# A causal convolution with 28 block products a tile in place of 31, and an S4 response whose tables move through the array

## The chip, the cores and the metric

The kernel runs on one core of one Trainium2 chip, as one launch. The time is the device time of one execution in microseconds, lower is better. A profile is one execution recorded by the hardware profiler; times inside it count from its first instruction. TensorE (PE) multiplies, VectorE (DVE) and ScalarE (ACT) work on what it leaves in PSUM, GpSimd (POOL) works on SBUF, and SyncE (SP) issues most DMAs.

## What is computed

One "macaron" layer on 2048 tokens of 1024 channels, all in float32: a feed-forward with 4-bit weights, a long convolution (S4), and the same feed-forward again.

```python
x = x + 0.5 * ffn(layernorm(x))        # ffn: silu(x @ Wg) * (x @ Wu) @ Wd, weights dequantized from 4 bits
x = x + s4(layernorm(x))
x = x + 0.5 * ffn(layernorm(x))

# s4, with L = 1024 and K the S4 response of length L, the same for all rows:
K = ifft(at_roots, L).real
y = irfft(rfft(u, n=2 * L) * rfft(K, n=2 * L), n=2 * L)[..., :L]
return y + D[0] * u
```

The S4 step is a causal convolution of each token's 1024 channels with K. With channels in eight blocks of 128 it is a block Toeplitz product: output block `i` is the sum over `j <= i` of input block `j` times T(i - j), where T(0) to T(7) are 128x128 matrices made from K.

## The kernel before

Tokens are worked in four blocks of 512 (four tiles of 128 each). `JOBS` lists eight feed-forwards, two for each block of tokens; the convolution of a block stands inside the job that follows its first feed-forward.

A job is `gate_up` and then `down`. `gate_up` runs 64 steps: eight waves of up to six PSUM accumulators (`pg`, units of 128 columns), eight groups of 128 input channels a wave. In a step each unit gets two products (L558): one with the float16 rest of the input (`xTl`), one with its high part (`xTh`). After each step but a wave's last, each accumulator is rescaled in place by the ratio of two quantization scales, by ScalarE for even units (L523) and by VectorE for odd ones (L525). After a wave's last step ScalarE makes `g` (L581), VectorE `hf` (L584, two buffers), and GpSimd splits that into `hh` (L586) and `hl` (L588). `down` works likewise with `po`.

Other work hangs on the steps as hooks. For the block of the job before, tile `t` is normalized at step 8 + 4t (L192), transposed in two halves at 10 + 4t (`turn_whole`, giving `st`), and convolved at 12 + 4t (`convolve`); in the first set all of that is 30 steps later, since the S4 tables come first (`s4_tables`, one piece a step of the second job). A scheduler of the language then puts the instructions of each engine in an order of its own, so the products of a convolution can be mixed with those of a step; an engine works through its queue in that order.

PSUM has eight banks: six accumulators and a pool of two (`bank`, tag `ps`), which transposes, convolution and tables share in turn. A bank can be written again when the engine that reads it is done.

`convolve` takes the lower four output blocks straight: four products, each of one input block with a run of `toeplitz`, in one bank (L898), which VectorE adds to `x` (L906). The upper four are done by pairs of blocks: GpSimd adds neighbouring input blocks (`sums`, L910), and three kinds of products (with `toeplitz` itself, and with `after` and `ahead`, differences of neighbouring T) fill a second bank, added at L933; those with `sums` fill a third, added to both blocks of a pair (L936). That is 31 block products in 17 instructions. A float32 product is recorded as two matmuls, each with its own weight load, so a group of 16 products counts x32.

`s4_response` (L829 to L852) makes K: 16 products, each with a 128x128 table (stride of eight columns) as weights and one column as moving operand, give K as 128 rows of eight, which are written to DRAM behind 127 zeros. `s4_toeplitz` reads that back so that row `p` is shifted by `p` (L869), turns the rows round with one product for each half (L872) and makes `toeplitz`, `after` and `ahead`.

Of the kernel before, what the change touches and what calls it, by code (L numbers as in the profile page):

```python
# [9 lines left out]
F32 = mybir.dt.float32  # L10
# [6 lines left out]
ALU = mybir.AluOpType  # L17
# [5 lines left out]
P = 128  # L23
HID = 1024
INTER = 2752
TOK = 2048
TB = 512
NT = TB // P
NC = HID // P
# [23 lines left out]
def macaron_s4_kernel(  # L53
# [31 lines left out]
    nc = tc.nc  # L85
# [4 lines left out]
    const = ctx.enter_context(tc.tile_pool(name="const", bufs=1))  # L90
# [7 lines left out]
    ypool = ctx.enter_context(tc.tile_pool(name="y", bufs=4))  # L98
# [4 lines left out]
    def bank(name):  # L103
        return ppool.tile([P, 512], F32, tag="ps", name=name)
# [4 lines left out]
    def t4(name):  # L109
        return xpool.tile([P, HID], F32, tag="x", name=name)  # L110

    def t2(name, dt=F32):
        return hpool.tile([P, 512], dt, tag="h", name=name)
# [28 lines left out]
    x = {}  # L142
# [376 lines left out]
    h = {}  # L519
# [125 lines left out]

    toeplitz = const.tile([P, HID], F32, tag="toeplitz", name="toeplitz")

    blocks = toeplitz.rearrange("p (d m) -> p d m", d=NC)  # L650
    after = const.tile([P, 3, P], F32, tag="after", name="after")
    ahead = const.tile([P, 3, P], F32, tag="ahead", name="ahead")
    k_dram = dpool.tile([1, P - 1 + HID], F32, tag="k", name="k_dram")
    s4 = {}

# [173 lines left out]
    def s4_response():  # L829

        tables = [t4("s4_tc"), t4("s4_ts")]
        for i in range(2):
            nc.sync.dma_start(tables[i], c_dft[:, i, :])
        ps = bank("s4_k")
        for r in range(8):
            for i in range(2):
                nc.tensor.matmul(
                    ps[:, r : r + 1],
                    tables[i].rearrange("p (a r) -> p r a", r=8)[:, r, :],
                    s4["se"][:, i, r : r + 1],  # L840
                    start=(i == 0),
                    stop=(i == 1),
                )
        k = t4("s4_response")
        d, none = k[:1, 8:9], k[:1, P : 2 * P - 1]
        nc.sync.dma_start(d, dskip.unsqueeze(0))
        nc.gpsimd.memset(none, 0.0)
        nc.vector.tensor_scalar(k[:, :8], ps[:, :8], 1.0 / HID, None, ALU.mult)
        nc.vector.tensor_tensor(k[:1, 0:1], k[:1, 0:1], d, ALU.add)
        nc.sync.dma_start(k_dram[:, : P - 1], none)  # L850
        nc.sync.dma_start(k_dram[0, P - 1 :].rearrange("(a r) -> a r", r=8), k[:, :8])
        s4.clear()  # L852

    def s4_toeplitz():

        both = [t4("s4_rows"), t4("s4_turn")]
        rows, turn = both[0], both[1][:, :P]
        nc.gpsimd.memset(turn, 0.0)
        nc.gpsimd.affine_select(
            out=turn,  # L860
            in_=turn,
            pattern=[[1, P]],
            compare_op=ALU.not_equal,
            fill=1.0,
            base=1 - P,
            channel_multiplier=1,
        )
        first = k_dram[:]
        nc.sync.dma_start(rows, bass.AP(first.tensor, first.offset, [[1, P], [1, HID]]))  # L869
        for i in range(NH):  # L870
            ps = bank(f"s4_t{i}")
            nc.tensor.matmul(ps, turn, rows[:, bass.ts(i, 512)], start=True, stop=True)  # L872
            dst = toeplitz[:, bass.ts(i, 512)]
            if i:
                nc.vector.tensor_copy(dst, ps)
            else:
                nc.scalar.copy(dst, ps)
        for dst, d in ((after, 3), (ahead, 1)):
            nc.vector.tensor_tensor(dst, blocks[:, d : d + 5 : 2], blocks[:, 2:7:2], ALU.subtract)

    def s4_tables():

        yield from s4_poles()
        yield
        yield from s4_roots()
        yield
        s4_response()
        yield
        s4_toeplitz()

    def convolve(b, t, s, name):

        ps = bank(f"pc_{name}_0")
        for c in range(4):
            nc.tensor.matmul(  # L898
                ps[:, P * c :],
                s[:, c, :],  # L900
                toeplitz[:, : 512 - P * c],
                start=(c == 0),
                stop=(c == 3),
            )
        part = x[b][t][:, :512]
        nc.vector.tensor_tensor(part, part, ps, ALU.add)  # L906

        sums = ypool.tile([P, TB], F32, tag="y", name=f"sums_{name}")
        sums = sums[:, : 3 * P].rearrange("p (c t) -> p c t", c=3)
        nc.gpsimd.tensor_tensor(sums, s[:, 0:6:2, :], s[:, 1:6:2, :], ALU.add)  # L910
        own = bank(f"pc_{name}_1")
        both = bank(f"pc_{name}_2")[:, : 2 * P].rearrange("p (y m) -> p y m", y=2)
        flat = own.rearrange("p (y m) -> p y m", y=4)
        upper, lower = flat[:, 0:4:2], flat[:, 1:4:2]

        def product(dst, lhsT, rhs, start=False, stop=False):
            nc.tensor.matmul(dst, lhsT, rhs, start=start, stop=stop, skip_group_check=True)  # L917

        for y in range(2):
            product(flat[:, 2 * y : 2 * y + 2], s[:, 4 + 2 * y, :], blocks[:, 0:2], start=(y == 0))  # L920
        for y in range(2):
            product(flat[:, 2 * y + 1], s[:, 5 + 2 * y, :], blocks[:, 0])
        for i in range(3):
            y = slice(max(0, i - 1), 2)
            d = slice(max(0, 1 - i), 3 - i)
            product(lower[:, y], s[:, 2 * i, :], after[:, d])
            product(upper[:, y], s[:, 2 * i + 1, :], ahead[:, d], stop=(i == 2))
        for i in range(3):
            y = slice(max(0, i - 1), 2)
            d = slice(2 * max(1, 2 - i), 2 * (3 - i) + 1, 2)  # L930
            product(both[:, y], sums[:, i, :], blocks[:, d], start=(i == 0), stop=(i == 2))
        part = x[b][t][:, 512:]
        nc.vector.tensor_tensor(part, part, own, ALU.add)  # L933
        part = part.rearrange("p (y h m) -> p y h m", y=2, h=2)
        twice = both.unsqueeze(2).to_broadcast([P, 2, 2, P])
        nc.vector.tensor_tensor(part, part, twice, ALU.add)  # L936

    def turn_whole(n, name):
        s = t4(name).rearrange("p (c t) -> p c t", c=NC)
# [12 lines left out]
    def general():  # L952
# [193 lines left out]
        for b in range(TOK // TB):  # L1146
            load_x(b, rows_of(u, b))
            feed_forward(b, 1)
            moments(b, 2)
            deviations(b, 2)  # L1150
            for t in range(NT):
                s = turn_whole(normalized(b, t), f"gt_{b}_{t}")
                convolve(b, t, s, f"g{b}_{t}")
            feed_forward(b, 3)
            for t, dst in enumerate(rows_of(out, b)):
                nc.sync.dma_start(dst, x[b][t])
            x.pop(b)
# [6 lines left out]
    def fast():  # L1164
        for j, (b, k) in enumerate(JOBS):
# [7 lines left out]
            if prev:  # L1173
# [3 lines left out]
                if pk == 1:  # L1177
# [11 lines left out]
                    def conv(t):  # L1189
                        convolve(pb, t, s4x.pop(t), f"{pb}_{t}")  # L1190
# [210 lines left out]
```

## Time and profile before

| | us |
|---|---|
| median of 4 runs | 2212.37 |
| lowest, highest | 2209.86, 2213.68 |
| the profiled execution | 2209.96 |
| its span, first to last instruction | 2208.2 |
| TensorE busy in it | 2123.3 |
| VectorE busy in it | 1702.4 |
| the 16 convolved tiles stand at | 465 to 518, 662 to 724, 1437 to 1499, 1713 to 1775 |
| the S4 response on TensorE | 423.8 to 433.5 |

Busy time is the time in which an engine has at least one instruction under way. Lengths of matmuls overlap, so the pace of TensorE is read from the starts. Idle time in brackets is that of the engine just before the instruction, with what ended it.

### The profile page before, as it was taken

To read this page: it belongs to the slowest core of one execution; us is meant where nothing else is said; L and a number is where in the kernel's file an instruction comes from. 1 tells how busy PE (TensorE), PEld (TensorE's weight loads), DVE (VectorE), ACT (ScalarE), POOL (GpSimd) and SP (SyncE) were. 2 spreads that over 40 slices of the span, in tenths; PEclk is the share of its full clock that TensorE was granted. 3 is DMA by queue.
4 is the path that set the end of the run, shared out by engine and by line. 5 is a ranking of instruction groups with operands and counts; after the bars stand their busy time and mean duration, and the time that the engine had idled before them with its cause. 6 is when DMAs were issued, how large, how long until landed. Compare 5 with 4: busy or idle time off the path is not lost.

```text
span 2208.2 us, 27967 instructions
## 1 busy us (share of the span) xinstructions
PE 2123.3 (96%) x9524; PEld 1416.3 (64%) x9524; DVE 1702.4 (77%) x2803; ACT 1425.0 (65%) x2245; POOL 367.5 (17%) x389
## 2 busy tenths in 40 slices
PE   5888899999999999999999999999999999999998
PEld 3454575566867558655785558676586765865576
DVE  7777968777786877778877788867788677777776
ACT  5677776555764577666766667646776467766675
POOL 0222302121011220122102220112201122012210
PEclk9999999999999999999999999999999999999999
DMA  7778774434453545644655455534445354564443
GB/s 246 250 244 283 240 252 150 140 103 154 138 156 115 169 134 157 192 142 123 206 172 163 127 169 138 153 115 157 135 137 153 115 177 136 155 196 142 132 132 121
DMA packets 163669, 359.93 MB, mean 163 GB/s; under 512 B 22395, under 2 KB 27572, under 8 KB 163518
## 3 DMA queue, kind: packets, MB, share of 16 engines
q1 hardware_dynamic: 162670, 356.50, 53.0%
q8 instruction: 78, 1.28, 0.2%
q10 hardware_dynamic: 592, 1.16, 0.1%
q0 software_dynamic: 256, 0.39, 0.1%
q14 instruction: 73, 0.60, 0.1%
HBM read 306.86 MB, written 50.73 MB: 162 GB/s over the span
## 4 chain that ended last, share of the span: by engine, by line
PE 54%; issue 24%; DVE 4%; POOL 4%; ACT 1%; DMA 1%; SPq 0%; POOLq 0%; DVEq 0%; ACTq 0%
PE pg L558 32%; PE po L620 16%; PE pc L917 3%; POOL hl L588 3%; DVE hf L584 2%; PE pc L898 1%; POOL hh L586 1%; DVE pg L525 1%; PE pb L641 1%; PE st L199 1%; PE pt L199 0%; ACT g L581 0%; DVE po L525 0%; DMA wd<-wdq 0%; DVE qd L470 0%
## 5 line engine op out<-in xcount | busy, mean ns | idle before, releaser
L523 ACT ACTIVATE pg<-pg,rat 128x512 f32<-128x512 f32 x1264 | 799.8, 660 | 475.9 <-PE pg L558 469.6
L525 DVE TENSOR_TENSOR pg<-pg,rat 128x512 f32<-128x512 f32 x1144 | 763.9, 694 | 184.1 <-PE pg L558 179.9
L558 PE MATMUL pg<-xTh,w 128*128 128x512 f32 x2752 | 882.0, 445 | 21.6 <-DVE hf L584 11.9
L558 PE MATMUL pg<-xTl,w 128*128 128x512 f16 x2752 | 745.4, 384 | 17.0 <-DMA w<-wq 9.3
L558 PEld LDWEIGHTS pg<-xTh,w 128*128 128x128 f32 x2752 | 521.0, 190 | 208.0 <-DVE hf L584 24.3
L620 PE MATMUL po<-hl,wd 128*128 128x512 f32 x1344 | 539.4, 403 | 13.1 <-DVE po L525 8.4
L523 ACT ACTIVATE po<-po,ratd 128x512 f32<-128x512 f32 x670 | 437.5, 662 | 166.4 <-PE po L620 166.0
L620 PE MATMUL po<-hh,wd 128*128 128x512 f32 x1344 | 524.6, 392 | 0.0
L525 DVE TENSOR_TENSOR po<-po,ratd 128x512 f32<-128x512 f32 x610 | 420.7, 697 | 99.5 <-PE po L620 95.3
L558 PEld LDWEIGHTS <-w 128*128 128x128 bf16 x2752 | 227.7, 99 | 360.2 <-issue 183.9
L586 POOL CAST hh<-hf 128x512 fp32r<-128x512 f32 x168 | 109.5, 652 | 1534.8 <-DVE hf L584 1452.2
L620 PEld LDWEIGHTS po<-hl,wd 128*128 128x128 f32 x1344 | 252.5, 188 | 91.7 <-DVE po L525 22.3
L620 PEld LDWEIGHTS po<-hh,wd 128*128 128x128 f32 x1344 | 253.7, 189 | 45.9
L588 POOL TENSOR_TENSOR hl<-hf,hh 128x512 fp32r<-128x512 f32 x168 | 222.2, 1322 | 13.4
L584 DVE SCALAR_TENSOR_TENSOR hf<-pg,rat,g 128x512 f32<-128x512 f32 x168 | 121.8, 746 | 92.4 <-ACT g L581 56.8
L581 ACT ACTIVATE g<-pg,rat 128x512 f32<-128x512 f32 x168 | 106.9, 686 | 64.2 <-PE pg L558 63.8
L162 DVE BATCH_NORM_STATS2 stats<-x 128x6 f32<-128x512 f32 x96 | 63.6, 677 | 1.1
L199 PE MATMUL pt<-ident,xn 128*128 128x128 f32 x256 | 43.0, 285 | 10.8 <-ACT xn L1269 10.8
L222 DVE TENSOR_TENSOR xTl<-pt,xTh 128x512 f16<-128x512 f32 x56 | 38.3, 688 | 14.2 <-ACT xTh L221 14.0
L643 DVE TENSOR_TENSOR x<-x,pb 128x512 f32<-128x512 f32 x64 | 43.2, 678 | 5.9 <-PE pb L641 5.0
L199 PEld LDWEIGHTS pt<-ident,xn 128*128 128x128 f32 x256 | 33.5, 147 | 21.3 <-ACT xn L1269 12.5
L641 PE MATMUL pb<-ident,y 128*128 128x128 f32 x256 | 42.5, 279 | 3.0 <-DVE x L643 2.9
(151 smaller groups left out, 808.6 us busy)
## 6 DMA issues: line engine op xcount, KB each, us to landing
w<-wq SPq DMA_DIRECT2D x319, 384.0 KB
wd<-wdq SPq DMA_DIRECT2D x336, 256.0 KB
w<-wq SPq DMA_DIRECT2D x128, 256.0 KB
w<-wq SPq DMA_DIRECT2D x64, 320.0 KB
x<-in_L_attn_u_dram SPq DMA_DIRECT2D x30, 512.0 KB
wq<-q SPq DMA_DIRECT2D x40, 384.0 KB
wdq<-qd SPq DMA_DIRECT2D x32, 256.0 KB
xs<-x SPq DMA_DIRECT2D x16, 512.0 KB
```

What stands on the lines that cost most here:

```text
L162: nc.vector.bn_stats(stats[:, t, i, :], x[b][t][:, bass.ts(i, 512)])
L199: nc.tensor.transpose(ps[:, bass.ts(k, P)], n[:, bass.ts(k, P)], ident)
L523: nc.scalar.activation(dst, src, AF.Copy, scale=sc)
L525: nc.vector.tensor_tensor(dst, src, sc.to_broadcast([P, TB]), ALU.mult)
L558: nc.tensor.matmul(p, weights, (lo, hi)[k][:, g, :], start=(g == 0 and not done), stop=(g == GK - 1 and done), skip_group_check=True,)
L581: nc.scalar.activation(g, pg, AF.Silu, scale=rat[:, 2 * f, GK - 1 :])
L584: nc.vector.scalar_tensor_tensor(hf, pu, last, g, ALU.mult, ALU.mult)
L586: nc.gpsimd.tensor_copy(hi, hf)
L588: nc.gpsimd.tensor_tensor(lo, hf, hi.bitcast(F32), ALU.subtract)
L620: nc.tensor.matmul(ps[c], w[:, bass.ts(c, P)], part, start=(f == 0 and k == 0), stop=(f == NF - 1), skip_group_check=True,)
L641: nc.tensor.transpose(ps[:, bass.ts(c, P)], yT[a, c][:, bass.ts(t, P)], ident)
L917: nc.tensor.matmul(dst, lhsT, rhs, start=start, stop=stop, skip_group_check=True)
```

## The change

`toeplitz` goes as a constant; in its place are `near` (T(0), T(1), T(2), T(4)), `after` and `ahead` with four blocks each, and `middle` (T(2) - T(4) and T(6) - T(4)). The lower four output blocks are now done by pairs too, and in the upper four the pairs with a whole distance between them are done by pairs of pairs, with further sums of input blocks. Each half uses a bank `pc` for what belongs to one block and a bank `pb` for what goes to several; VectorE adds five times a tile.

The response is made as one row: the one column is the weight, the table is the moving operand, 128 columns a product, in two banks; K then goes to DRAM as one row of 4 KB.

```diff
-    toeplitz = const.tile([P, HID], F32, tag="toeplitz", name="toeplitz")
-    blocks = toeplitz.rearrange("p (d m) -> p d m", d=NC)
-    after = const.tile([P, 3, P], F32, tag="after", name="after")
-    ahead = const.tile([P, 3, P], F32, tag="ahead", name="ahead")
+    near = const.tile([P, 4, P], F32, tag="near", name="near")
+    after = const.tile([P, 4, P], F32, tag="after", name="after")
+    ahead = const.tile([P, 4, P], F32, tag="ahead", name="ahead")
+    middle = const.tile([P, 2, P], F32, tag="middle", name="middle")
...
-        ps = bank("s4_k")
-        for r in range(8):
-            for i in range(2):
-                nc.tensor.matmul(
-                    ps[:, r : r + 1],
-                    tables[i].rearrange("p (a r) -> p r a", r=8)[:, r, :],
-                    s4["se"][:, i, r : r + 1],
...
+        for half in range(2):
+            ps = bank(f"s4_k{half}")
+            for r in range(4):
+                for i in range(2):
+                    nc.tensor.matmul(
+                        ps[:1, bass.ts(r, P)],
+                        s4["se"][:, i, 4 * half + r : 4 * half + r + 1],
+                        tables[i].rearrange("p (a r) -> p r a", r=8)[:, 4 * half + r, :],
...
-        nc.sync.dma_start(k_dram[0, P - 1 :].rearrange("(a r) -> a r", r=8), k[:, :8])
+        nc.sync.dma_start(k_dram[:, P - 1 :], k[:1])
...
+        nc.vector.tensor_copy(near[:, 0:3], blocks[:, 0:3])
+        nc.vector.tensor_copy(near[:, 3], blocks[:, 4])
         for dst, d in ((after, 3), (ahead, 1)):
-            nc.vector.tensor_tensor(dst, blocks[:, d : d + 5 : 2], blocks[:, 2:7:2], ALU.subtract)
+            own = dst[:, 0:3]
+            nc.vector.tensor_tensor(own, blocks[:, d : d + 5 : 2], blocks[:, 2:7:2], ALU.subtract)
+            nc.vector.tensor_tensor(dst[:, 3], dst[:, 2], dst[:, 1], ALU.subtract)
+            nc.vector.tensor_tensor(dst[:, 2], dst[:, 0], dst[:, 1], ALU.subtract)
+        for i in range(2):
+            src = blocks[:, 2 + 4 * i]
+            nc.vector.tensor_tensor(middle[:, i], src, blocks[:, 4], ALU.subtract)
...
+        nc.gpsimd.tensor_tensor(sums[:, 0:3], s[:, 0:6:2, :], s[:, 1:6:2, :], ALU.add)
+        nc.gpsimd.tensor_tensor(quad, s[:, 0:2, :], s[:, 2:4, :], ALU.add)
+        nc.gpsimd.tensor_tensor(sums[:, 3], sums[:, 0], sums[:, 1], ALU.add)
...
+        for o in range(2):
+            own = bank(f"pc_{name}_{o}")
+            flat = own.rearrange("p (d m) -> p d m", d=4)
+            mine = s[:, 4 * o : 4 * o + 4]
+            product(flat[:, 0:2], mine[:, 0], near[:, 0:2], start=True)
+            product(flat[:, 1], mine[:, 1], near[:, 0])
+            product(flat[:, 2:4], mine[:, 2], near[:, 0:2])
+            product(flat[:, 3], mine[:, 3], near[:, 0])
+            product(flat[:, 3], mine[:, 0], after[:, 0])
+            product(flat[:, 2], mine[:, 1], ahead[:, 0], stop=(o == 0))
+            both = bank(f"pb_{name}_{o}")
+            if o == 0:
+                product(both[:, :P], sums[:, 0], near[:, 2], start=True, stop=True)
+            else:
+                for y in range(2):
+                    product(flat[:, 2 * y + 1], s[:, 2 - 2 * y], after[:, 2 + y])
+                    product(flat[:, 2 * y], s[:, 3 - 2 * y], ahead[:, 2 + y], stop=(y == 1))
+                twice = both.rearrange("p (y m) -> p y m", y=4)
+                product(twice[:, 0], sums[:, 1], middle[:, 0], start=True)
+                product(twice[:, 1], sums[:, 0], middle[:, 1])
+                product(twice[:, 1], sums[:, 2], near[:, 2])
+                for y in range(2):
+                    product(twice[:, y], sums[:, 3], near[:, 3])
+                product(twice[:, 3], quad[:, 0], after[:, 1])
+                product(twice[:, 2], quad[:, 1], ahead[:, 1], stop=True)
+            part = x[b][t][:, bass.ts(o, 512)]
+            nc.vector.tensor_tensor(part, part, own, ALU.add)
+            part = part.rearrange("p (y h m) -> p y h m", y=2, h=2)
+            if o == 0:
+                part = part[:, 1]
+                add = both[:, :P].unsqueeze(1).to_broadcast([P, 2, P])
+                nc.vector.tensor_tensor(part, part, add, ALU.add)
+            else:
+                add = twice[:, 0:2].unsqueeze(2).to_broadcast([P, 2, 2, P])
+                nc.vector.tensor_tensor(part, part, add, ALU.add)
+                add = twice[:, 2:4].unsqueeze(1).to_broadcast([P, 2, 2, P])
+                nc.vector.tensor_tensor(part, part, add, ALU.add)
```

In the changed kernel the add of `pc` is L949, that of the first `pb` L954, those of the second L957 and L959.

More of the change, by code (lines that the diff above doesn't have):

```diff
@@ L833, in s4_response @@
             nc.sync.dma_start(tables[i], c_dft[:, i, :])
-        ps = bank("s4_k")
-        for r in range(8):
-            for i in range(2):
-                nc.tensor.matmul(
-                    ps[:, r : r + 1],
-                    tables[i].rearrange("p (a r) -> p r a", r=8)[:, r, :],
-                    s4["se"][:, i, r : r + 1],
[L841 to L845, printed above, removed]
+        k, rest = t4("s4_response"), t2("s4_rest")
+        d, none = rest[:1, :1], rest[:1, 1:P]
         nc.sync.dma_start(d, dskip.unsqueeze(0))
         nc.gpsimd.memset(none, 0.0)
-        nc.vector.tensor_scalar(k[:, :8], ps[:, :8], 1.0 / HID, None, ALU.mult)
+        for half in range(2):
[6 more added lines that the diff above has]
+                        tables[i].rearrange("p (a r) -> p r a", r=8)[:, 4 * half + r, :],
+                        start=(i == 0),
+                        stop=(i == 1),
+                    )
+            nc.vector.tensor_scalar(
+                k[:1].rearrange("p (a r) -> p r a", r=8)[:, 4 * half : 4 * half + 4],
+                ps[:1].rearrange("p (r a) -> p r a", r=4),
+                1.0 / HID,
+                None,
+                ALU.mult,
+            )
         nc.vector.tensor_tensor(k[:1, 0:1], k[:1, 0:1], d, ALU.add)
         nc.sync.dma_start(k_dram[:, : P - 1], none)
-        nc.sync.dma_start(k_dram[0, P - 1 :].rearrange("(a r) -> a r", r=8), k[:, :8])
+        nc.sync.dma_start(k_dram[:, P - 1 :], k[:1])
         s4.clear()
     def s4_toeplitz():
-        both = [t4("s4_rows"), t4("s4_turn")]
-        rows, turn = both[0], both[1][:, :P]
+        rows, turn, whole = t4("s4_rows"), t4("s4_turn")[:, :P], t4("s4_whole")
         nc.gpsimd.memset(turn, 0.0)
@@ L872, in s4_toeplitz @@
             nc.tensor.matmul(ps, turn, rows[:, bass.ts(i, 512)], start=True, stop=True)
-            dst = toeplitz[:, bass.ts(i, 512)]
+            dst = whole[:, bass.ts(i, 512)]
             if i:
@@ L877, in s4_toeplitz @@
                 nc.scalar.copy(dst, ps)
+        blocks = whole.rearrange("p (d m) -> p d m", d=NC)
+        nc.vector.tensor_copy(near[:, 0:3], blocks[:, 0:3])
+        nc.vector.tensor_copy(near[:, 3], blocks[:, 4])
         for dst, d in ((after, 3), (ahead, 1)):
-            nc.vector.tensor_tensor(dst, blocks[:, d : d + 5 : 2], blocks[:, 2:7:2], ALU.subtract)
+            own = dst[:, 0:3]
[5 more added lines that the diff above has]
+            nc.vector.tensor_tensor(middle[:, i], src, blocks[:, 4], ALU.subtract)
     def s4_tables():
@@ L891, in convolve @@
     def convolve(b, t, s, name):
[L896 to L906, printed above, removed]
-        sums = ypool.tile([P, TB], F32, tag="y", name=f"sums_{name}")
-        sums = sums[:, : 3 * P].rearrange("p (c t) -> p c t", c=3)
@@ L910, in convolve @@
[L910 to L914, printed above, removed]
+        sums = ypool.tile([P, TB], F32, tag="y", name=f"sums_{name}")
+        sums = sums.rearrange("p (c t) -> p c t", c=4)
+        quad = ypool.tile([P, TB], F32, tag="y", name=f"quad_{name}")
@@ L916, in product @@
+        quad = quad[:, : 2 * P].rearrange("p (c t) -> p c t", c=2)
+        nc.gpsimd.tensor_tensor(sums[:, 0:3], s[:, 0:6:2, :], s[:, 1:6:2, :], ALU.add)
+        nc.gpsimd.tensor_tensor(quad, s[:, 0:2, :], s[:, 2:4, :], ALU.add)
+        nc.gpsimd.tensor_tensor(sums[:, 3], sums[:, 0], sums[:, 1], ALU.add)
         def product(dst, lhsT, rhs, start=False, stop=False):
             nc.tensor.matmul(dst, lhsT, rhs, start=start, stop=stop, skip_group_check=True)
-        for y in range(2):
-            product(flat[:, 2 * y : 2 * y + 2], s[:, 4 + 2 * y, :], blocks[:, 0:2], start=(y == 0))
@@ L921, in convolve @@
[L921 to L936, printed above, removed]
+        for o in range(2):
[35 more added lines that the diff above has]
+                nc.vector.tensor_tensor(part, part, add, ALU.add)
```

## The prediction

> **What bounds the kernel now.** I read the page first: TensorE is busy for 96% of the span, VectorE for 77%.
>
> ```profile
> PE 2123.3 (96%) x9524; PEld 1416.3 (64%) x9524; DVE 1702.4 (77%) x2803; ACT 1425.0 (65%) x2245; POOL 367.5 (17%) x389
> ```
>
> So a change pays if it shortens TensorE's own queue and adds no wait to it. Next the timeline around one of the 16 convolved tiles (TensorE, then VectorE). Columns: start, length, engine, line, what, count.
>
> ```profile
> 662.37 2.32 PE L898 MATMUL pc<-toeplitz,st 128*128 128x512 f32 x8
> 664.53 1.47 PE L917 MATMUL pc<-toeplitz,st 128*128 128x256 f32 x8
> 665.84 0.60 PE L917 MATMUL pc<-after,st 128*128 128x256 f32 x2
> 666.27 0.60 PE L917 MATMUL pc<-ahead,st 128*128 128x256 f32 x2
> ...
> 667.57 0.39 PE L917 MATMUL pc<-after,st 128*128 128x128 f32 x2
> 667.79 0.39 PE L917 MATMUL pc<-ahead,st 128*128 128x128 f32 x2
> 668.01 1.25 PE L917 MATMUL pc<-toeplitz,sums 128*128 128x256 f32 x6
> 669.10 0.81 PE L558 MATMUL pg<-xTl,w 128*128 128x512 f16 x3
> ```
>
> ```profile
> 664.73 0.69 DVE L906 TENSOR_TENSOR x<-x,pc 128x512 f32<-128x512 f32 x1 [1.29 <-PE pc L898]
> 665.45 0.69 DVE L162 BATCH_NORM_STATS2 stats<-x 128x6 f32<-128x512 f32 x1
> 668.21 0.69 DVE L933 TENSOR_TENSOR x<-x,pc 128x512 f32<-128x512 f32 x1 [2.07 <-PE pc L917]
> ```
>
> Starts, not lengths, give the pace: a product of 256 columns takes 0.433 us (665.84 to 666.27), one of 128 takes 0.22 (667.57, 667.79, 668.01). The tile occupies TensorE from 662.37 to 669.10, 6.73 us for 31 blocks, without a gap: the bank of L898 is added by VectorE while L917 runs in the other bank. VectorE begins that add 0.42 us after the start of the last L898 product (664.31) and ends at 665.42.
>
> Half of the later tiles look different: the step ahead of them ends a wave, and VectorE first owes three `hf` products, the third of which waits for GpSimd.
>
> ```profile
> 680.60 1.41 DVE L584 SCALAR_TENSOR_TENSOR hf<-pg,rat,g 128x512 f32<-128x512 f32 x2 [1.47 <-ACT g L581]
> 683.40 0.75 DVE L584 SCALAR_TENSOR_TENSOR hf<-pg,rat,g 128x512 f32<-128x512 f32 x1 [1.40 <-POOL hl L588]
> 684.07 0.68 DVE L906 TENSOR_TENSOR x<-x,pc 128x512 f32<-128x512 f32 x1
> ```
>
> That convolution starts at 680.77, so its first bank is free only 3.98 us later. Before, nothing needs the bank until the last group of products at 686.41.
>
> **The change part by part: products of a tile.** 17 products become 24: four of 256 columns, 20 of 128. 4 x 0.433 + 20 x 0.22 = 6.13 us against 6.73: 0.6 us less a tile, 16 tiles, 9.6 us if nothing waits.
>
> Narrow products in long runs are new: before, at most two follow each other. The nearest row is L764: 16 weight loads of 128 columns, each with a product of 8 columns, start 0.111 us apart, and a 128-column f32 product is two such loads, so 0.22 holds. I take it. The Trainium skill (TensorE: Matmul & The Clock Gate, Back-to-back issue gap) says the spacing of load and product pairs is set by both, and gives 81 ns a pair at 128 columns where the product alone would take about 56. By that ratio 20 products would take 6.4 us instead of 4.4 and the tile would lose; this trace's 0.22 beside 0.433 does not agree.
>
> **The two banks.** A tile now uses four banks out of a pool of two: `pc_0`, `pb_0`, `pc_1`, `pb_1`. `pc_1` can't start until VectorE has added `pc_0` (L949). The built program's order of instructions shows what stands between: the one product of `pb_0` and three gate/up products (five or six in the tiles behind a wave's end). On TensorE the weight stream queues behind that wait. Per tile, from the tile's first product:
>
> Ten tiles (four in the first set, six later): `pc_0` takes 2 x 0.433 + 4 x 0.22 = 1.75; its last product starts at 1.53, the add runs 0.42 later, 1.95 to 2.64; releases by VectorE reach TensorE 0.06 later (hf L584 ends at 441.44, the product starts at 441.49), so 2.70. TensorE has work until 1.75 + 0.22 + 3 x 0.2155 = 2.62. Wait 0.08. Then `pc_1` 2 x 0.433 + 8 x 0.22 = 2.63 and `pb_1` 7 x 0.22 = 1.54: done at 6.87. Before, the same work (tile and three products) took 6.73 + 0.65 = 7.38. Gain 0.5.
>
> Six tiles behind a wave's end: VectorE's queue puts the add behind the three `hf`, as before, so it ends at 3.98, and `pc_1` starts at 4.04. TensorE has work until 1.75 + 0.22 + 5 x 0.2155 = 3.05. Wait 1.0. Done at 4.04 + 2.63 + 1.54 = 8.21, against 6.73 + 5 x 0.2155 = 7.81. Loss 0.4.
>
> Sum: -10 x 0.5 + 6 x 0.4 = -2.6 us. Most of the gain goes into the wait.
>
> `pb_1` needs the add of `pb_0` (256 columns, under 0.69 us, behind L949): ready by 3.4, needed at 5.3. No wait.
>
> **VectorE and GpSimd.** Adds go from three to five a tile (four of 0.69, one of 256 columns), up to 1.1 us more of VectorE. Between two tiles TensorE runs some 48 products and transposes, about 11 us; VectorE has 12 rescales, a copy, a normalization, statistics and two adds there, 0.6 to 0.7 us each when back to back (the statistics at 665.45 follow the add at 664.73), some 10.5 us. It fits, with under 1 us to spare; I take 0, bounds 0 to 0.3 a tile. GpSimd gets two more sums a tile (256 and 128 columns; L910 takes 1.0 us for 384, so about 1 us). In the later tiles it sits idle there until the `hf` arrive 4 us later; nothing.
>
> **The S4 response.** Once only. Before, 16 products of one column each load a 128x128 table with stride 8 (lengths min/median/max, first and last start):
>
> ```profile
> L837 PE MATMUL s_k<-s_work,s_tc x16: 187/376/378, 423.8 to 432.8; 128*128 128x1 f32 x16
> ```
>
> Their 32 records start 0.238 us apart, 7.2 us in all; and then TensorE crawls, as the windows show (PE, PEld, DVE, ACT, POOL busy, then the granted clock):
>
> ```profile
> 426.50:433.40 6.90, 6.90 (x31) 6.90 (x31) 0.70 (x1) 0.66 (x1) 0.00 (x0) 0.77 0.00 0
> 433.40:436.80 3.40, 3.40 (x9) 1.61 (x10) 0.91 (x3) 0.00 (x0) 0.00 (x0) 0.50 0.40 117
> ```
>
> The 14 products from 433.48 to 438.07 take 4.6 us where 14 x 0.225 = 3.15 is usual: 1.45 us lost to the clock.
>
> After, the response value is the one-column weight and the table moves, 128 columns with the same stride. No row shows a strided moving operand. Bounds: 0.111 a record (unstrided weights, L764), 0.238 (the same tables, strided, as weights). I take 0.238, the row of the same reads: 7.6 us, 0.4 more. The clock: columns now stream, and I take it that it stays up, -1.45; bounds 0 and -1.45. The skill (same page, What's actually happening) says the throttle is let go by activity and comes back after an idle window of about 3.4 us. Here it came back with TensorE's records filling 6.90 of 6.90 us, so busy records are not what is counted. By the page alone rival 3 below could not happen; by this row it can.
>
> VectorE gains two writes of 512 (0.69 each for 0.17) and, for the tables, copies and differences worth about 2 us (L879 takes 0.55 for 384 columns, so at most that for each smaller one). Rescales wait behind them; the built order fills with products of the units that ScalarE rescales. I take 0.3, bounds 0 and 3. The Toeplitz rows: one write of 4 KB for 128 of 32 bytes, then the load, which landed 4.7 us after its issue at 438.69, just ahead of its use at 443.50. The issue is still held behind a weight load that waits for the step's end, and the use is still some 24 products later, so it moves along: 0, bound 1.
>
> S4 sum: +0.4 - 1.45 + 0.3 = -0.75.
>
> **Sum.** -2.6 - 0.75 = -3.35 us. The profiled run took 2209.96 (span 2208.2 and 1.8 around it), 2206.6 after; it lies 2.4 under the median of 2212.37, so the median goes to 2209.0, -0.15%. About 0.2% (4.4 us) is what a measurement of this kernel can tell from no change.
>
> **The rivals.**
> 1. The table streams at full pace: 32 x 0.111 = 3.6, so -3.65 instead of +0.4; total -2.6 - 3.65 - 1.45 + 0.3 = -7.4, 2205.0. For: the operand's pace is 0.108 a record unstrided. Against: the 0.238 of the same reads.
> 2. Slower: in all 16 tiles the first add comes as late as behind a wave's end. VectorE has 1.1 us more a tile; if its backlog at a tile's start reaches 3.3 us, the add ends at 3.98 everywhere. For: the margin above is under 1 us. Against: before, its last rescale ends 1.07 us into the tile, and the add waits 1.29 us for TensorE. Price: 16 x 0.4 = +6.4, S4 -0.75: 2218.0. It decides from an add that ends later than 3.2 us after the first product: there the gain of 0.5 is gone.
> 3. The clock falls all the same, only one column of the array being in use: -2.6 + 0.4 + 0.3 = -1.9, 2210.5.
> 4. Long runs of narrow products are load bound (a load's record lasts 0.19 us): 20 x 0.38 + 1.73 = 9.3 a tile, +2.6, 16 tiles +41: 2250. Against: the 16 loads of L764. The skill's ratio above would be a milder form of it.
>
> **How the numbers follow.** Forecast 0.42, rivals 0.24, 0.18, 0.12, 0.04. Faster by over 0.2% means under 2208.0: most of rival 1 and the quarter of the forecast in which the windows come out a microsecond better, 0.35. Slower means above 2216.8: two thirds of rival 2, rival 4 and a little of the unknown VectorE backlog, 0.21. The rest 0.44. The range reaches from rival 1 with 1.5 us of bounds, 2203.5, to rival 2 with one, 2219.0.
>
> **What would show it.** In the profile after: `pc` products of 128 columns 0.22 apart; the idle time of TensorE ahead of the second `pc` group, released by VectorE, 0.1 us in ten tiles and 1.0 in six; the pace of the `s_k` records (0.11 or 0.24); a granted clock of 1.0 behind them. Waits of 1 us in every tile, or paces off 0.22, would make it wrong.

## The result, and the profile after

The changed kernel takes 2210.51 us (median of 34 runs, 2205.2 to 2215.37), the kernel before 2213.34 (55 runs, 2209.45 to 2218.68): ratio 0.9986, 95% interval 0.9981 to 0.9991. By the ratio that is 3.1 us less (2.0 to 4.2), by the medians 2.8: a small gain, below the 0.2% that the prediction counted as a change. The forecast was 3.35 less, and 2209.0. The profiled execution took 2213.24 (span 2211.5), which is 3.3 us more than that of before; the table further down shows that none of that lies in changed work.

First the page, engine by engine (busy time, share of the span, instructions).

```profile
PE 2121.3 (96%) x9748; PEld 1419.3 (64%) x9748; DVE 1715.7 (78%) x2844; ACT 1425.8 (64%) x2245; POOL 387.6 (18%) x421
```

TensorE has 224 more matmul records (14 a tile) and yet 2.0 us less busy time. The timeline of a tile that does not follow a wave's end, TensorE and then VectorE (start, length, engine, line, what, count, in brackets the idle time before it):

```profile
665.58 1.47 PE L921 MATMUL pc<-near,st 128*128 128x256 f32 x8
666.89 0.39 PE L921 MATMUL pc<-after,st 128*128 128x128 f32 x2
667.11 0.39 PE L921 MATMUL pc<-ahead,st 128*128 128x128 f32 x2
667.33 0.39 PE L921 MATMUL pb<-near,sums 128*128 128x128 f32 x2
667.56 0.81 PE L558 MATMUL pg<-xTl,w 128*128 128x512 f16 x3
668.28 1.58 PE L921 MATMUL pc<-near,st 128*128 128x256 f32 x8
...
672.51 1.63 PE L558 MATMUL pg<-xTh,w 128*128 128x512 f32 x6
```

```profile
667.53 0.69 DVE L949 TENSOR_TENSOR x<-x,pc 128x512 f32<-128x512 f32 x1 [0.89 <-PE pc L921]
668.33 0.42 DVE L954 TENSOR_TENSOR x<-x,pb 128x256 f32<-128x256 f32 x1
```

The narrow products start 0.22 apart (666.89, 667.11, 667.33, 667.56), as forecast. The second `pc` bank starts at 668.28, 2.70 after the tile's first product, just behind the add of the first bank (1.95 to 2.64). The tile and its three gate/up products are done after 6.93.

A tile behind a wave's end, VectorE and then TensorE:

```profile
686.26 0.75 DVE L584 SCALAR_TENSOR_TENSOR hf<-pg,rat,g 128x512 f32<-128x512 f32 x1 [1.40 <-POOL hl L588]
686.93 0.68 DVE L949 TENSOR_TENSOR x<-x,pc 128x512 f32<-128x512 f32 x1
```

```profile
683.62 1.47 PE L921 MATMUL pc<-near,st 128*128 128x256 f32 x8
...
685.59 0.81 PE L558 MATMUL pg<-xTl,w 128*128 128x512 f16 x3
686.05 0.82 PE L558 MATMUL pg<-xTh,w 128*128 128x512 f32 x2
687.66 1.57 PE L921 MATMUL pc<-near,st 128*128 128x256 f32 x8 [0.78 <-DVE x L949]
...
691.89 1.17 PE L558 MATMUL pg<-xTh,w 128*128 128x512 f32 x4
```

The add waits behind the `hf` that waits for GpSimd; the bank is free at 687.61, 3.99 after the tile's start, and TensorE starts the second bank at 687.66. The 0.78 in brackets counts from the modelled end of the product before; by the pace of the starts, which is how the forecast counts, the wait is 0.97. The trace's list of TensorE's waits between 640 and 1800 us (what waited for what: total, times, longest) has this at its head; before, the line wasn't there.

```profile
PE pc L921 <- DVE x L949: 4.5, 6, 0.8
```

The response, as the tile's instructions (min/median/max ns, first and last start), and in windows (PE, PEld, DVE, ACT, POOL busy, granted clock, DMA):

```profile
L843 PE MATMUL s_k<-s_tc,s_work x16: 389/411/412, 429.9 to 439.0; 128*1 128x128 f32 x16
L850 DVE TENSOR_SCALAR s_response<-s_k x2: 1059/1072/1084, 436.7 to 439.9; 1x512 f32<-1x512 f32 x2
```

```profile
436.00:439.70 3.70, 3.70 (x17) 1.54 (x15) 1.21 (x2) 0.00 (x0) 0.00 (x0) 1.00 0.00 0
439.70:443.00 3.30, 3.15 (x14) 1.83 (x14) 1.68 (x2) 1.34 (x3) 0.00 (x0) 1.00 0.41 115
```

The records start 0.232 us apart, near the 0.238 of before, and the clock behind them stays at 1.00 where it had been 0.50.

Where the time went is read from the start of the same VectorE instruction (an `hf` or a `y`) in both profiles, after less before. The convolved tiles are taken as four sets of four, one set for each block of tokens:

| at, before | what lies up to it | later in the changed kernel by | change |
|---|---|---|---|
| 358.08 | opening, no changed instruction | +6.12 | |
| 462.67 | S4 tables and response | +5.26 | -0.86 |
| 585.44 | first four tiles | +3.20 | -2.06 |
| 769.98 | second four | +2.66 | -0.54 |
| 1360.72 | no tile | +2.96 | +0.30 |
| 1635.77 | third four | +3.09 | +0.13 |
| 1818.18 | last four | +3.29 | +0.20 |
| 2195.58 | no tile | +3.23 | -0.07 |

From 358 us on the changed kernel gains 2.9 us, about what the medians show; the changed stretches alone gain 3.1. How exact this reading is, three more kernels with the same convolution tell (experiments 1, 4 and 7): their four sets change by -2.05 to -2.20, -0.34 to -0.51, +0.01 to +0.11 and +0.04 to +0.15. So a set is known to about 0.2 us, while a long stretch without a tile can differ by 0.4. The opening differs by up to 6.1 us between the profiled executions; it hides the gain in this pair of profiles, and that is why the experiments below are read from 358 us on as well as by their medians.

### The profile page after: what moved, and what is told of

The parts are those of the page before. It is cut to its first block, busy times and chain, and to the rows that moved or that the text cites. A ratio compares the mean times of both kernels' runs of the same rounds, so it can differ in the third digit from the quotient of the medians.

```text
span 2211.5 us, 28501 instructions
## 1 busy us (share of the span) xinstructions
PE 2121.3 (96%) x9748; PEld 1419.3 (64%) x9748; DVE 1715.7 (78%) x2844; ACT 1425.8 (64%) x2245; POOL 387.6 (18%) x421
## 4 chain that ended last, share of the span: by engine, by line
PE 54%; issue 23%; DVE 4%; POOL 4%; ACT 1%; DMA 1%; SPq 0%; DVEq 0%; POOLq 0%; ACTq 0%
PE pg L558 32%; PE po L620 16%; POOL hl L588 3%; PE pc L921 3%; DVE hf L584 2%; POOL hh L586 1%; PE pb L921 1%; DVE pg L525 1%; PE pb L641 1%; PE st L199 1%; ACT g L581 1%; PE pt L199 0%; DMA wd<-wdq 0%; DVE po L525 0%; DMA s_cos<-in_c_rows_dram 0%
## 5 line engine op out<-in xcount | busy, mean ns | idle before, releaser
L586 POOL CAST hh<-hf 128x512 fp32r<-128x512 f32 x168 | 109.1, 650 | 1528.6 <-DVE hf L584 1429.1
L588 POOL TENSOR_TENSOR hl<-hf,hh 128x512 fp32r<-128x512 f32 x168 | 222.5, 1324 | 13.3
L921 PE MATMUL pc<-near,st 128*128 128x256 f32 (+1 forms) x256 | 49.2, 333 | 4.5 <-DVE x L949 4.5
L921 PEld LDWEIGHTS pc<-near,st 128*128 128x128 f32 x256 | 42.3, 190 | 16.0 <-DVE x L949 10.8
```

The source lines that it names most:

```text
L586: nc.gpsimd.tensor_copy(hi, hf)
L588: nc.gpsimd.tensor_tensor(lo, hf, hi.bitcast(F32), ALU.subtract)
```

## The experiments

The theory on trial is the prediction's: 9.6 us of products are saved, most of that is given back to the wait for the first `pc` bank, and the response gains only through the clock. All ratios are to the kernel before, with 95% intervals.

**1. The convolution alone.** New convolution, old response:

```diff
+                    ps[:, r : r + 1],
+                    tables[i].rearrange("p (a r) -> p r a", r=8)[:, r, :],
+                    s4["se"][:, i, r : r + 1],
...
-                        ps[:1, bass.ts(r, P)],
-                        s4["se"][:, i, 4 * half + r : 4 * half + r + 1],
-                        tables[i].rearrange("p (a r) -> p r a", r=8)[:, 4 * half + r, :],
```

> The changed convolution with the S4 response of before. Theory (the parts add up: the convolution gives 2 us, the response 0.9): ratio to before 0.9990 or 0.9991; in the profile the products of the response start 0.238 us apart, the granted clock falls to about 0.5 behind them, and the second bank of a tile waits 0.1 us in ten tiles and 0.95 in six. Rival (the gain is the response's alone, the convolution is a wash): 1.0000, with the same waits, and the windows of the 16 tiles no shorter than before.

Measured 2210.82 (11 runs), ratio 0.9992 (0.9983 to 1.0001). Same tiles as in the changed kernel: 6.90 or 8.23 us to the last record's start, waits of 0.07 and 0.95. The clock falls to one half again (the first window holds records of the response, the second the last of them and the gate/up products behind):

```profile
430.00:434.20 4.20, 4.20 (x20) 4.20 (x19) 0.56 (x1) 0.66 (x1) 0.00 (x0) 1.00 0.00 0
434.20:441.00 6.80, 6.80 (x22) 4.82 (x23) 0.91 (x3) 0.57 (x1) 0.00 (x0) 0.51 0.20 58
```

One more thing shows: the load of the Toeplitz rows comes too late here, by the 1.1 us that the prediction gave as its upper bound and took at zero.

```profile
448.07 1.96 PE L872 MATMUL s_t<-s_rows,s_turn 128*128 128x512 f32 x4 [1.08 <-DMA s_rows<-k_dram]
```

Here, and in experiment 7, which also has the old response with the new convolution, the wait is there; before and in the changed kernel it is not. In this pair the instruction that issues the load (L869) lasts 1.57 and 1.59 us, before and in the changed kernel 0.37; what holds it up was not traced. By the landmarks the late load costs 1.6 us, while the four sets of tiles gain 2.5: the convolution gives its 2 us, as the theory said and against the rival, though the median alone could not tell.

**2. The response alone.** Old convolution, new response (against the kernel before):

```diff
-                    ps[:, r : r + 1],
-                    tables[i].rearrange("p (a r) -> p r a", r=8)[:, r, :],
-                    s4["se"][:, i, r : r + 1],
...
+                        ps[:1, bass.ts(r, P)],
+                        s4["se"][:, i, 4 * half + r : 4 * half + r + 1],
+                        tables[i].rearrange("p (a r) -> p r a", r=8)[:, 4 * half + r, :],
```

> The convolution of before with the new response. Theory (parts add up): ratio 0.9996; products of the response 0.232 us apart, the clock stays at 1.0 behind them, about 0.9 us won between the start of the response and the Toeplitz product. Rival (the gain is the response's alone): 0.9987.

Measured 2212.03 (11 runs), ratio 0.9994 (0.9985 to 1.0004). From the first `s_k` record to the `hf` that starts at 437.87 before, 14.08 us before and in experiment 1, it takes 13.24 here, in the changed kernel 13.23, and 13.24 in experiments 3 and 5. So the new response gains 0.84 by itself, to the hundredth in every trace. In this trace and in that of experiment 5 the stretch ahead of it, from the last `hf` but one before the response, takes 17.7 us instead of 16.9, so that this trace gains only 0.2 us from 358 us on. TensorE waits there 0.62 and 0.38 us for two rescales on VectorE (0.61 and 0.38 in experiment 5), where before it waits 0.14 and 0.15. VectorE's order of instructions in that stretch is the same, but three of its small S4 operations (L794, 128x8) last 0.63 to 0.83 us and not 0.15, where before two do, and each of the long ones ends 0.02 us behind a GpSimd instruction beside it (L586 or L588). So a few hundredths of a microsecond in the starts seem to decide this, not the edit. The medians of 1 and 2 alone are 2.2 and 1.0 under that of before, together 3.2, where both parts in one kernel give 2.8; neither interval excludes no change.

**3. The order of the banks.** Both `pc` first, then `pb_1`, then `pb_0`; all products, adds and banks are the same:

```diff
+        own = [bank(f"pc_{name}_{o}") for o in range(2)]
         for o in range(2):
-            own = bank(f"pc_{name}_{o}")
...
-            both = bank(f"pb_{name}_{o}")
...
+        both = bank(f"pb_{name}_1")
...
+        both = bank(f"pb_{name}_0")
```

> The changed kernel with the four banks of a tile taken in the order pc_0, pc_1, pb_1, pb_0, so that 2.6 us of products stand between the end of pc_0 and the reuse of its bank; same products, same adds. Theory (the wait of TensorE for VectorE's first add is where the gain of three blocks went): no wait in any tile, 6.13 to 6.2 us a tile, 16 x 0.6 and 0.85 of the response, ratio 0.9953. Rival (VectorE's five adds a tile are the limit, and the wait comes back ahead of the next steps' rescaled banks): ratio 0.9985, with idle time of TensorE released by L525 behind each tile.

Measured 2203.7 (5 runs, 2201.82 to 2207.64), ratio 0.9959 (0.9944 to 0.9974). The same tile behind a wave's end as above, TensorE and then VectorE:

```profile
679.95 1.47 PE L921 MATMUL pc<-near,st 128*128 128x256 f32 x8
...
685.92 0.39 PE L921 MATMUL pb<-near,sums 128*128 128x128 f32 x2
686.14 0.81 PE L558 MATMUL pg<-xTl,w 128*128 128x512 f16 x3
```

```profile
683.25 0.68 DVE L938 TENSOR_TENSOR x<-x,pc 128x512 f32<-128x512 f32 x1
684.56 0.69 DVE L938 TENSOR_TENSOR x<-x,pc 128x512 f32<-128x512 f32 x1 [0.62 <-PE pc L921]
```

The add comes as late as ever (3.30 after the start), but the first bank is now asked for only at 684.36, with `pb_1`; the tile runs without a gap and occupies TensorE for 6.19 us (679.95 to 686.14). That is the pace of the products undisturbed, forecast 6.13. The waits for the first bank are gone from all tiles, which shows that they came from the order of the banks; the rival's 0.9985 lies outside the interval. One new wait comes up, in the last tile of the second set:

```profile
723.99 0.49 PE L921 MATMUL pb<-near,sums 128*128 128x128 f32 x2 [2.17 <-DVE x L938]
```

There VectorE has work on the next job's scales queued (L341, L368, L344, L345, from 719.65 on), so the add of the second bank ends at 723.94, and `pb_0`, which takes that bank, waits. The wait costs more than its 2.17 us, since the granted clock falls behind it (the third number from the right):

```profile
724.00:728.00 4.00, 4.00 (x12) 2.67 (x13) 3.06 (x7) 1.32 (x2) 0.00 (x0) 0.58 0.18 74
```

The trace has it at one half for 3.4 us from 724.64 on, which loses an estimated 1.7 us more (half of 3.4). Experiment 6 has the same wait and the same fall (0.59 from 720 to 724 us).

From 358 us on this trace gains 5.5 us on that of before, 2.6 more than the changed kernel. By sets it gains 2.7, loses 0.7 where the wait and the slow clock are, and gains 1.8 and 1.5. So the theory is right on the wait and too high on the sum: it had 9.6 us from the tiles. Its median gains 9.3, with an interval from 5.8 to 12.4: the trace speaks for the lower end.

**4. The stride of the table.** The constant is stored so that the 128 columns of a product lie side by side:

```diff
-                        tables[i].rearrange("p (a r) -> p r a", r=8)[:, 4 * half + r, :],
+                        tables[i][:, bass.ts(4 * half + r, P)],
...
+    dft = dft.reshape(P, 2, P, 8).transpose(0, 1, 3, 2).reshape(P, 2, L)
```

> The changed kernel with the table of the response laid out so that the 128 columns of a product lie side by side (its constant is stored in that order); nothing else. Theory (the stride of eight columns sets the pace of 0.232 us a record): records 0.111 us apart, 3.6 us in place of 7.5, ratio to before 0.9969. Rival (a one-column weight or the float32 moving operand sets the pace): 0.232 again, ratio 0.9986.

Measured 2204.81 (6 runs), ratio 0.9963 (0.995 to 0.9976). The record is shorter, and the stretch from the first `s_k` record to the same `hf` takes 9.30 us, 3.93 less than in the changed kernel:

```profile
L843 PE MATMUL s_k<-s_tc,s_work x16: 270/272/273, 427.6 to 433.3; 128*1 128x128 f32 x16
```

The records start 0.109 apart. So the operand's stride alone made the difference between rival 1 and the forecast. The Trainium skill (Advanced Engine Details and Errata, Memory Cachelines) says that on-chip memory is read in lines of 16 bytes and that an access to another line each time is penalized; the columns here were 32 bytes apart, and these runs put the price at 0.232 against 0.109 us a record. From 358 us on this trace gains 7.4 us.

**5. The convolution one step later.** No tile then stands directly behind the three `hf`:

```diff
-                        at(up, late + 12 + 4 * t, lambda t=t: conv(t))
+                        at(up, late + 13 + 4 * t, lambda t=t: conv(t))
```

> The convolution of a tile is entered one step later in the order of the work, so that three gate/up products instead of five stand between the two banks and no tile begins directly behind the three hf products that end a wave; nothing else is changed. Theory (the 0.95 us waits of six tiles come from VectorE's queue at the end of a wave: two hf, one that waits for GpSimd, then the add of pc_0): the add ends at 2.64 us in these tiles too, pc_1 starts at 2.70, and 6 x 0.9 = 5.4 us come back, about 2207.6, ratio 0.9962 to the kernel before where the changed kernel has 0.9986. Rival (the products of the tile were what TensorE did while the hf chain ran; moved away, the chain makes the next gate/up product wait instead): the wait shows up as pg on hf or on the rescale at L525, as long as before, and the time stays at 2210 to 2211, ratio 0.9986.

Measured 2213.79 (12 runs), ratio 1.0008 (1.0 to 1.0017). The theory of this experiment fell, and the rival was right in kind. The tile that stood behind a wave's end now looks like this on TensorE:

```profile
685.05 0.82 PE L921 MATMUL pc<-near,st 128*128 128x256 f32 x4
685.92 0.50 PE L558 MATMUL pg<-xTh,w 128*128 128x512 f32 x1
686.26 0.39 PE L558 MATMUL pg<-xTl,w 128*128 128x512 f16 x1
686.49 0.82 PE L921 MATMUL pc<-near,st 128*128 128x256 f32 x4
...
688.53 1.57 PE L921 MATMUL pc<-near,st 128*128 128x256 f32 x8
```

The wait ahead of the second `pc` bank is 0.07, as the theory said. But the gate/up product that needs the late accumulator now waits itself, as the trace's list for 640 to 1800 us says, which had 2.8 us in 11 waits on that line in the changed kernel:

```profile
PE pg L558 <- DVE hf L584: 5.4, 17, 1.5
PE pc L921 <- DVE x L949: 1.3, 1, 1.3
```

3.2 us less ahead of `pc`, 2.6 us more ahead of `pg`. In the third and fourth set the landmarks move as in the changed kernel, within 0.1 us: per set the list has 1.5 us less ahead of `pc` and 0.8 more ahead of `pg` on `hf`, and the landmarks show no gain at all. There the rival's price is right.

The second set loses 1.9 us more, and not for the rival's reason alone. Ahead of its last tile VectorE stands for 3.20 us in front of an instruction of the next job's scales that waits for GpSimd (1.13 us in the changed kernel), the `hf` behind it come late, and TensorE waits for them; this is the 1.5 in the list above. VectorE, then TensorE:

```profile
720.77 0.14 DVE L367 TENSOR_SCALAR want<-row_t 32x1 f32<-32x1 f32 x1 [3.20 <-POOL row_t L355]
```

```profile
721.65 0.38 PE L558 MATMUL pg<-xTl,w 128*128 128x512 f16 x1 [1.46 <-DVE hf L584]
```

In the last tile the add of the first bank then meets the rest of that work: the second line of the list, 1.3 us in one wait. Of the 3.3 us between this median and that of the changed kernel the traces show 2.9 from 358 us on: 0.8 ahead of the response (experiment 2), 0.4 in the first set and 1.9 in the second, with 0.2 back elsewhere. So the median says little about the tiles behind a wave's end; the third and fourth set do.

**6. Experiments 3 and 4 together.**

> Both edits that gained by themselves: the banks in the order pc_0, pc_1, pb_1, pb_0, and the response tables stored so that the 128 columns of a product lie side by side. Theory (the wait for the first add and the stride of the moving operand are two separate costs, in two separate stages): the gains add, 2203.7 and 2204.8 against 2210.5, so 2198.0, ratio 0.9932. Rival (part of each gain is the variation of the opening stage, or what one gives is taken by the waits of the next stage): no better than the better of the two, 2203 to 2204, ratio 0.996.

Measured 2202.06 (6 runs, 2200.27 to 2204.61), ratio 0.9955 (0.9942 to 0.9968): better than both kernels, and short of the 2198.0 that the sum of medians promised. The traces tell which part of the sum was wrong. From 358 us on the gains over the changed kernel are 2.6 (experiment 3), 4.5 (experiment 4) and 7.3 (both): they do add. The response takes 9.30 us as in 4, the tiles 6.08 us to the last record's start as in 3, and the 2.2 us wait is there too. What did not add is the part of experiment 3's median that its trace doesn't have, as the rival said of the opening.

**7. The old response, with the table side by side.** Experiment 1 with the table of experiment 4, as weights:

```diff
-                    tables[i].rearrange("p (a r) -> p r a", r=8)[:, r, :],
+                    tables[i][:, bass.ts(r, P)],
```

> New convolution with the old response (the tables are the weights, one column moves), but with the tables stored contiguously, so that each record should take 0.111 instead of 0.238 us. Theory (the granted clock falls because a stretch of one-column products leaves TensorE's array all but empty for long, 7.5 us, and half as long a stretch lets it fall less or not at all): the 32 records take 3.6 us, the clock in the windows behind them stays above 0.9, and the time is 3.9 to 5.4 us under the 2210.8 of the new convolution with the old response, 2205.4 to 2206.9, ratio 0.9966 to 0.9972. Rival (any run of one-column products brings the clock to one half, however short): the windows behind the records show 0.5 for 3 us or more again, and the gain is 3.9 or a little less. Third (the stride is not what makes a record take 0.238 us): no gain at all, ratio 0.9990.

Measured 2207.8 (12 runs), ratio 0.9982 (0.9973 to 0.9992), 3.0 under experiment 1. The records start 0.112 apart, so the stride also made the old weights slow. The clock falls all the same, for half as long:

```profile
432.00:435.70 3.70, 3.70 (x33) 3.55 (x32) 0.70 (x1) 0.78 (x2) 0.00 (x0) 1.00 0.03 12
435.70:439.20 3.50, 3.50 (x10) 1.79 (x9) 0.91 (x3) 0.26 (x1) 0.00 (x0) 0.51 0.41 114
```

The theory said above 0.9, and was wrong; the rival said 0.5 for 3 us or more with a gain of 3.9 or a little less, and is the nearer. From the first `s_k` record to the same `hf` it takes 10.05 us, 4.03 less than in experiment 1. A row of one-column products that lasts 3.3 us is long enough to bring the clock down, and the fall costs about as much as before: the second window counts 10 matmuls in 3.5 us, the slow window before 9 in 3.4. In the long row the first half of the slow spell lay under the one-column records themselves, and their 0.238 us did not change when the clock fell.

## Why the prediction came out right, by its steps

**Pace of the products: right, 0.06 short.** 6.13 us a tile forecast, 6.19 measured where nothing waits (experiment 3). The gain is 0.54 a tile rather than 0.6, since a narrow product takes 0.223 and not 0.22. The long runs of narrow products are not load bound: rival 4 is out, and the ratio of 81 to 56 ns that the Trainium skill (TensorE: Matmul & The Clock Gate, Back-to-back issue gap) gives for 128 columns has no counterpart in these float32 pairs.

**The wait for the first bank: right in place, time and price.** Six tiles behind a wave's end: `pc_1` forecast at 4.04 and found at 4.02 to 4.08 after the start, wait (by the starts) 0.94 to 0.97 in five of them and 0.77 in the last of the second set, where the forecast said 1.0; done at 8.25 to 8.31, forecast 8.21. The other tiles of the later sets: 2.70 forecast and found, wait 0.07 where 0.08 was forecast, done at 6.93 where 6.87 was. The small excess is 0.1 us that TensorE loses once more behind the wait. By sets, the first gained 2.06 (forecast 2.0), the others 0.54, -0.13 and -0.20 (forecast 0.2 each). The sum for the 16 tiles, 2.27 by the table, was forecast at 2.6. Part of that closeness is luck: the second set does better than the third and fourth because the kernel before has a wait at its end that the forecast didn't list, for a rescale behind VectorE's work on the next job's scales, and the changed kernel has only 0.22 us of it:

```profile
729.11 0.59 PE L558 MATMUL pg<-xTl,w 128*128 128x512 f16 x2 [1.75 <-DVE pg L525]
```

In the first set the way there was another: the first product of three tiles starts early, gate/up products stand behind it, the add ends at 4.0 to 4.6 and the tiles last 8.3 to 8.9 (gate/up products among them included). The waits are short there (0.3) because other work fills in. The forecast had these among the tiles without a late add; the sum of the set was right by luck, the picture of those three tiles was not.

**VectorE and GpSimd at nothing: right.** The add of `pb_0` ends 0.5 us after that of `pc_0` and nobody waits for it. Rival 2 needed an add ending later than 3.2 us in all tiles; in the later sets that holds for the tiles behind a wave's end and for no other.

**The response: -0.86 measured, -0.75 forecast, with two terms off.** The pace of the strided operand, taken from the row of the same reads as weights, was near (0.232 against 0.238, so +0.2 for the +0.4 of the sum), and experiment 4 shows that it was the stride. The clock stayed up, which rules out rival 3. The two writes of the response were sized at 0.69 each and took 1.07; they write one partition with a stride of eight. With -1.45 for the clock that leaves some +0.4 for VectorE's work, where the sum had +0.3; this is a remainder, no run measures it alone. TensorE went on beside them: in the last window shown it is busy for 3.15 of 3.30 us.

**The DMA of the Toeplitz rows at nothing: right here, and close to wrong.** Experiments 1 and 7 show a wait of 1.1 us, about the 1 that was its bound.

**The median.** The forecast took 3.35 us from the 2212.37 of the four runs; over 55 runs the kernel before has 2213.34. The 1.5 us between 2209.0 and 2210.51 are that (1.0) and a gain of 2.8 by the medians for 3.35 (0.5); of the latter the table puts 0.3 in the tiles.

## What to carry to other kernels

A saving in products is worth what the next wait leaves of it: list for each buffer who must be done before it is written again, and put as much work as there is between the two. Here the same products in another order of banks were worth about as much as the change itself (2.6 us by the traces, beside 2.9); moving the tile away from the late add was worth nothing, because the tile had been covering a wait that then showed. And look at what a new wait does to the clock: the one wait of 2.17 us that the better order left cost an estimated 1.7 us on top.

An operand that is read with a stride is worth a look at every use, as weights as well as moving: storing a constant in another order added no instruction and gained more (3.9 us) than the change had.

When an opening that waits for memory varies by several us, compare two profiles from a landmark behind it, and by stretches that are alike in kernels that should not differ there.

## What the runs showed of the hardware

- **The clock falls under full records.** In 3.3 to 7 us of one-column products TensorE's records fill the windows, and the granted clock goes to 0.50, 3.5 to 4.4 us after the row of products begins (before, and experiments 1 and 7). The same sums with 128 moving columns, at the same pace, leave it at 1.00. The low spells last 6.8, 6.8 and 3.4 us. The Trainium skill (TensorE: Matmul & The Clock Gate, What's actually happening) gives a window of about 3.4 us and two rates, full and half; the spells agree with one or two such windows. By its rule an idle window brings the clock down; here it was a busy one with almost nothing streaming.
- **The clock also falls behind a wait of 2.2 us.** In experiments 3 and 6 TensorE waits 2.17 us once among its products, and the granted clock goes to one half for 3.4 us behind it. A wait of 1.75 us before (at 729.11) and of 1.46 us in experiment 5 left it at 1.00. Where between them the limit lies, and what else it depends on, these runs don't show.
- **Stride, in numbers.** A record with 128 float32 columns 32 bytes apart takes 0.232 us as moving operand and 0.238 as weights, side by side 0.109 and 0.112.
- **A strided write on VectorE.** 512 values written to one partition, 32 bytes apart, take 1.07 us (L850), where an add of 128x512 with the values side by side takes 0.69 (L949). The two differ in more than the stride, and no run separates it.
